# Chained instruction orders on four engines, and paired sums, in the delta-rule stage of a perceiver block

## The chip, the cores and the metric

The kernel runs on one core of a Trainium2 chip. The metric is device time in microseconds (us), the median of several runs. The engines are named as the profile names them: PE (TensorE; PEld is its weight loading), DVE (VectorE), ACT (ScalarE), POOL (GpSimd) and SP (SyncE, which here only issues DMAs).

## What is computed

`x` has 128 sequences of 32 tokens with 512 features, in all 4096 rows. Three blocks follow each other, each as `x = x + block(layernorm(x))`: a cross attention, a delta-rule layer with an MLP, and a quantised Hadamard feed-forward. The change touches the delta-rule layer, whose first half is, cut to what matters:

```python
h = _rms(x, attn_norm_w)
q = silu(silu(_causal_dwconv(h @ Wq.T, conv_q)))
k = silu(silu(_causal_dwconv(h @ Wk.T, conv_k)))
v = silu(silu(_causal_dwconv(h @ Wv.T, conv_v)))
q = _l2norm(q.reshape(B, T, nh, hd))     # 32 heads of 16
k = _l2norm(k.reshape(B, T, nh, hd))
beta = sigmoid(h @ Wbeta.T)
def step(S, inp):
    kt, qt, vt, bt = inp
    err = einsum('bhvk,bhk->bhv', S, kt) - vt
    S = S - bt[..., None, None] * err[..., None] * kt[..., None, :]
    o = einsum('bhvk,bhk->bhv', S, qt)
    return (S, o)
```

Then come an RMS norm, an output projection and an MLP of 1408 units.

## The kernel before, in words

**Stages.** Rows are handled in 8 groups (`NG`) of 512 rows (`SG`), that is, 16 sequences. `cross_attention` writes its result `x1` to DRAM. `delta_products` (L602) makes q, k, v, their products and lengths. `delta_out_mlp` (L923) makes the layer's output and the MLP in 16 blocks of 256 rows; `HadamardFfn` follows. The recurrence is not run token by token: within a sequence the products k·k and k·q of all token pairs are formed on PE, and a forward substitution over the 32 tokens (`Substitution.solve`, L513, on DVE) yields the vectors that the state would have been updated with. Products go to DRAM as `ld` (k·k) and `pd` (k·q, with the causal mask), values as `vd`, the solution as `ud`, the lengths of q as `rq`.

**A group's round.** `a_round` (L808) has twelve steps: k and q for each of four blocks of 128 channels, then v for the four. A step's parts are these. `channels` (L656): 4 matmuls into `pp` (three PSUM banks), an ACT copy with the last tap into `acc`, three DVE instructions for the other taps (L667). `activated` (L676): two SiLUs on ACT for the *preceding* step's `acc`; after a q step the pair k, q of that channel block is ready, and `masked` has two pieces of 256 rows queued. `hold` (L688): for up to three pieces ahead, eight DMAs on SP (`masked_operand`, L553, issued at L558) copy k and q head by head into one of three zeroed tiles `kqm`. `multiply` (L695), in eight of twelve steps (`due`): 32 PE instructions into the two `pg` banks, two ACT copies into `kk`, the mask on POOL, and POOL's DMAs to `ld` and `pd` (`products`, L561). In steps 3, 5, 7 and 9 ACT squares a pair, and in steps 4, 6, 8 and 10 `add` (L721) sums the squares by head on PE into three strips of 32 rows of the bank `pn`, the middle strip being the logits of beta. Step 11 takes roots and tanh (`lengths`, L731). In steps 7 to 10 `normed` (L647) normalises a tile of the next group on DVE (`hn`), transposes it on PE and copies it on ACT. For the group before, `behind_round` (L786) transposes lengths and beta (`by_tokens`, step 1) and values (`put_v`, steps 2 to 5), and inverts the lengths of q (`inverted`, steps 8 and 10; its load `rl` on SP at L594). `last_round` (L854) does the same for group 7, with the channels in the order k, v, q.

**Beside it.** `mixed` draws from the round and from the substitution in proportion to their estimated costs: `SHARE`, 24.3 us, per round, from group 1 on, the first 12.15 of it empty. `solve` loads a group's `ld` in four quarters into L (one buffer, 512 KB a quarter, L520) and `vd` into W (two buffers, L526). For each token there are a small product (L535), a product `pr` (L539) and a subtraction (L545), on 31 to 1 tokens. The rest of the substitution runs beside the MLP.

**Who orders.** The order in which an engine gets its instructions is fixed when the kernel is built: a scheduler takes them by program order, and may put a later one ahead when its own reckoning has the engine free. `InOrder` wraps an engine and ties each instruction that goes through it to the one before, so that their program order stays. Before the change PE and ACT are wrapped in this stage; DVE, SP and POOL are not. The matmul order, say, is therefore the written one, whereas a substitution step or a load can be put ahead of what is written before it.

**Start.** `scaled_rows` (L495) multiplies the 16 strips of `wk`, `wq`, `wv` and `wb` by the norm's weights on DVE (L502), written ahead of the first four `normed`. POOL zeroes the tiles `um` and `pe` of the next stage (L1528); `kqm` is zeroed on DVE, four strips a step (L831).

The lines that fix a step's order, from `a_round`:

```python
acc, last = channels(hT, n, ec)
with tc.issue_after(last):
    for _ in range(min(H4, len(blank))):
        nc.vector.memset(blank.pop(0), 0.0)
activated()
waiting.append((acc, dst, masked(ec) if n == "q" else kept))
if due[j] and count["done"] < len(held) and (old or j >= 4):
    multiply()
```

Of the kernel before, what the change touches and what calls it, by code (L numbers as in the profile page):

```python
# [494 lines left out]
def scaled_rows(nc, wp, name, norm, ws, engine=None):  # L495

    mul = engine.mul if engine else nc.vector.tensor_scalar_mul
    nw = wp.tile([P, DC], FP, name=name, bufs=1)
    nc.sync.dma_start(nw, norm.rearrange("(c p) -> p c", p=P))
    for t in ws:  # L500
        for dc in range(DC):
            mul(t[:, dc, :], t[:, dc, :], nw[:, dc : dc + 1])  # L502


class Substitution:
# [4 lines left out]
    def __init__(self, g, pool, ld, vd, ud):  # L510
        self.nc, self.pool, self.ld, self.vd, self.ud = g.nc, pool, ld, vd, ud

    def solve(self, gi):  # L513
# [5 lines left out]
        def load(s):  # L519
            nc.sync.dma_start(  # L520
                L[:, s : s + some].rearrange("p s h t -> p s (h t)"), rows[:, s : s + some]
            )
# [3 lines left out]
        nc.sync.dma_start(  # L526
# [5 lines left out]
        for s in range(T):  # L532
            if s % some == 0 and s + some < T:
                load(s + some)
            nc.vector.tensor_mul(w[:, s], w[:, s], bc(W[:, s, :, HD], HD))  # L535
            n = T - 1 - s
            if n:
                pr = self.pool.tile([P, T - 1, H4, HD], FP, name="pr")
                nc.vector.tensor_mul(  # L539
                    pr[:, 0:n],  # L540
                    bc(L[:, s, :, s + 1 : T].rearrange("p h t -> p t h"), HD),
                    w[:, s].unsqueeze(1).to_broadcast([P, n, H4, HD]),
                )
                yield 0.3 + 0.07 * n
                nc.vector.tensor_sub(w[:, s + 1 :], w[:, s + 1 :], pr[:, 0:n])  # L545
# [7 lines left out]
def masked_operand(nc, m, kq):  # L553


    for h in range(HH):
        rows = slice(h * HD, (h + 1) * HD)
        nc.sync.dma_start(m[rows, h % H4], kq[rows])  # L558
# [31 lines left out]
def inverted(nc, rq, r):  # L590
# [3 lines left out]
    nc.sync.dma_start(r, every)  # L594
    yield
    nc.vector.tensor_scalar_max(r, r, 1e-12)
    nc.vector.reciprocal(r, r)
# [4 lines left out]
def delta_products(  # L602
    g: Ctx, x1, stats, norm_w, wqT, wkT, wvT, conv_q, conv_k, conv_v, wbT, heads, causal, ld, vd,
    pd, rq, kd, beside,
# [16 lines left out]
    act = InOrder(tc, nc.scalar)  # L621
    with stack:
# [13 lines left out]
        scaled_rows(nc, wp, "nw", norm_w, [w["k"], w["q"], w["v"], w["b"]])  # L636

        kqm = [wp3.tile([P, H4, 2, KT], FP, name=f"kqm{i}") for i in range(3)]
        blank = [t[:, h] for t in kqm for h in range(H4)]
        mv, rs = stats  # L640

        def load(n):
            xt = xp.tile([P, D], FP, name="xt")
            nc.sync.dma_start(xt, x1[n * P : (n + 1) * P, :])
            return xt

        def normed(n, xt, hT):  # L647

            i = n % GT
            hn = hp.tile([P, D], FP, name="hn")  # L650
            nc.vector.tensor_scalar(
                hn, xt, mv[:, n, 0:1], rs[:, n, 1:2], ALU.subtract, ALU.mult
            )
            act.copy(hT[:, :, i * P : (i + 1) * P], g.transposed(ps, hn, g.ident, pe=pe))

        def channels(hT, n, ec):  # L656
# [9 lines left out]
            for d in range(1, TAPS):  # L666
                last = nc.vector.scalar_tensor_tensor(  # L667
# [3 lines left out]
            return acc.rearrange("p b t -> p (b t)"), last.ins  # L671
# [16 lines left out]
        def hold():  # L688
            while len(held) < min(len(pieces), count["done"] + len(kqm)):
                gi, ec, half, kq = pieces[len(held)]  # L690
                m = kqm[len(held) % len(kqm)]
                masked_operand(nc, m, kq[:, :, half * KT : (half + 1) * KT])
# [13 lines left out]
        class Group:  # L706

            def __init__(self, gi):  # L710
                self.gi = gi
                self.sums = psn.tile([3 * H, SG], FP, name="pn")
                self.v = {}

            def square(self, kq, of="kq"):
# [3 lines left out]
                return sq  # L719

            def add(self, sq, hT, ec, of="kq"):  # L721
                at = dict(start=ec == 0, stop=ec == DC - 1)
                if "k" in of:
                    pe.matmul(self.sums[0:H], hs[:, ec, :], sq[:, 0], **at)
                    pe.matmul(
                        self.sums[H : 2 * H], w["b"][:, ec, :], hT[:, ec, :], **at
                    )
                if "q" in of:
                    return pe.matmul(self.sums[2 * H :], hs[:, ec, :], sq[:, 1], **at)

            def lengths(self, of="kq"):  # L731

                if "k" in of:
                    f = self.factors = wk.tile([3 * H, SG], FP, name="f", bufs=1)
                    act.activation(f[H : 2 * H], self.sums[H : 2 * H], AF.Tanh, scale=0.5)
                for n, r in (("k", slice(0, H)), ("q", slice(2 * H, 3 * H))):
                    if n in of:
                        act.activation(self.factors[r], self.sums[r], AF.Sqrt)

            def by_tokens(self):  # L740
                f = self.factors
                pt = ps.tile([P, GT, 2 * H], FP, name="ps")
                for i in range(GT):
                    pe.transpose(
                        pt[:, i, :], f[0 : 2 * H, i * P : (i + 1) * P], g.ident[0 : 2 * H, 0 : 2 * H]
                    )
                self.n = st.tile([P, GT, H], FP, name="n")
                nc.vector.tensor_scalar_max(self.n, pt[:, :, 0:H], 1e-12)
                self.beta = st.tile([P, GT, H], FP, name="beta")
                nc.vector.tensor_scalar(self.beta, pt[:, :, H:], 0.5, 0.5, ALU.mult, ALU.add)  # L750
                n2 = st.tile([P, GT, H], FP, name="n2", bufs=1)
                nc.vector.tensor_mul(n2, self.n, self.n)
                nc.vector.reciprocal(n2, n2)
                nc.vector.tensor_mul(self.beta, self.beta, n2)

            def put_q(self):

                for c in range(DC):
                    rows = slice(2 * H + c * HH, 2 * H + (c + 1) * HH)
# [5 lines left out]
            def put_v(self, ec):  # L765
# [6 lines left out]
                nc.vector.tensor_mul(  # L772
# [13 lines left out]
        def behind_round(old, j):  # L786
# [4 lines left out]
            if j == 1:  # L791
# [3 lines left out]
                    nc, rq[old.gi], st.tile([P, P], FP, name="rl", bufs=1)  # L795
# [10 lines left out]
        loads = (2, 3, 4, 8)  # L806

        def a_round(gi, old, hT, made):  # L808
# [12 lines left out]
            for j, (n, ec) in enumerate(todo):  # L821
# [6 lines left out]
                acc, last = channels(hT, n, ec)  # L828
                with tc.issue_after(last):
                    for _ in range(min(H4, len(blank))):  # L830
                        nc.vector.memset(blank.pop(0), 0.0)  # L831
                activated()
                waiting.append((acc, dst, masked(ec) if n == "q" else kept))
                if due[j] and count["done"] < len(held) and (old or j >= 4):
                    multiply()
                if 3 <= j <= 9 and j % 2:
                    sq = new.square(kq[(j - 3) // 2])
                if 4 <= j <= 10 and j % 2 == 0:
                    new.add(sq, hT, (j - 4) // 2)
# [4 lines left out]
                if j == 11:  # L844
                    new.lengths()
                if 7 <= j <= 10:
                    normed((gi + 1) * GT + j - 7, xt[j - 7], hT_next)
# [6 lines left out]
        def last_round(gi, old, hT):  # L854
# [8 lines left out]
            for j, (n, ec) in enumerate((n, ec) for n in "kvq" for ec in range(DC)):  # L863
# [7 lines left out]
                acc, _ = channels(hT, n, ec)  # L871
                if (n, ec) == ("q", DC - 2):
                    left["q"] = [
                        i for i in nc.cur_bb.bb.instructions[before:] if i.engine == pe.last.engine
                    ][:1]
                activated()
                waiting.append((acc, dst, stored(ec) if n == "q" else kept))
                if count["done"] < len(held):
                    multiply()
                if 3 <= j <= 6:  # L880
                    new.add(sq, hT, j - 3, "k")
                if 2 <= j <= 5:
                    sq = new.square(kq[j - 2], "k")
                if j == 7:
                    new.lengths("k")
# [7 lines left out]
                if j == 11:  # L893
                    new.add(sq, hT, 0, "q")
                if j >= 10:
                    sq = new.square(kq[j - 10], "q")
# [3 lines left out]
            for ec in range(1, DC):  # L900
                if ec > 1:
                    sq = new.square(kq[ec], "q")
                sums = new.add(sq, hT, ec, "q").ins
                if ec > 1:
                    left["pe"].append(sums)
# [3 lines left out]

        hT = wk1.tile([P, DC, SG], FP, name="hT")  # L910
        for i in range(GT):
            normed(i, load(i), hT)
# [707 lines left out]
```

## Time and profile before

| what | value |
|---|---|
| runs, median of 3 | 2903.06 us (2902.81 to 2907.43) |
| profiled execution | 2912.17 us, of which the span is 2910.4 us |
| busy over the span | PE 2815.8 us (97%), PEld 1676.1, DVE 1995.4 (69%), ACT 1034.9 (36%), POOL 741.5 (25%) |
| granted PE clock, mean | 0.989 |
| first and last `pp` matmul | 686.3 and 1194.9 us |
| `pn` matmuls (sums and logits) | 192 instructions of 128x512, median 617 ns |
| substitution steps L539 and L545, whole span | 248 each, 307.6 and 308.1 us |

The span is the time from the first to the last instruction on the core. The time of an execution has a little around it. In a view's row, `out<-in` are the kernel's tile names, `xN` the number of instructions, and the bracket tells how long the engine stood idle before the row and whose end released it. A matmul of float32 takes two instructions, which is why a step's 4 matmuls appear as x8. A busy PE in the profile is not necessarily PE at full rate, since the ends of matmuls are modelled and the granted clock varies.

### The profile page before, as it was taken

The numbers are of one execution on the slowest core, as the hardware profiler recorded it, in microseconds if no ns is written. First come the engines' busy times: TensorE is split into PE (matmuls) and PEld (weight loads), VectorE is DVE, ScalarE is ACT, GpSimd is POOL, SyncE is SP. The second block draws the span as 40 slices with busy tenths as digits, with TensorE's granted clock in tenths as the row PEclk, the third lists the DMA queues.
The fourth block names the chain that finished last, engine by engine and source line by source line (L and its number), as shares of the span: only waits on it lengthen the run. The fifth ranks groups of instructions, "written<-read, shape, count | busy, mean of one in ns | idle before, by whom it ended". The sixth has DMA issues, their size and how long they took to land.

```text
span 2910.4 us, 44713 instructions
## 1 busy us (share of the span) xinstructions
PE 2815.8 (97%) x16726; PEld 1676.1 (58%) x16726; DVE 1995.4 (69%) x3355; ACT 1034.9 (36%) x1794; POOL 741.5 (25%) x1102
## 2 busy tenths in 40 slices
PE   8999999997999899999999999999999999999998
PEld 4444444443434344567666767776776756666665
DVE  2453544425599895678787878887722279999997
ACT  1111111213666466522212221211221147677665
POOL 2232323322777677221212111101000000000000
PEclk9999999998999899999999999999999999999999
DMA  9898998873555545841414141413231124444443
GB/s 317 268 321 296 345 334 291 302 248 87 163 161 144 167 135 155 236 137 57 131 57 132 57 132 54 123 59 94 69 112 33 35 73 83 90 88 82 87 81 71
DMA packets 347176, 429.77 MB, mean 148 GB/s; under 512 B 151888, under 2 KB 252624, under 8 KB 344528
## 3 DMA queue, kind: packets, MB, share of 16 engines
q1 hardware_dynamic: 305952, 324.36, 37.0%
q0 software_dynamic: 41008, 102.55, 11.6%
q8 instruction: 133, 2.18, 0.3%
q14 instruction: 83, 0.68, 0.1%
HBM read 288.88 MB, written 94.37 MB: 132 GB/s over the span
## 4 chain that ended last, share of the span: by engine, by line
PE 58%; DVE 11%; issue 2%; DMA 2%; POOL 2%; ACT 1%; SPq 1%; ACTq 0%; DVEq 0%; POOLq 0%
PE ps L151 18%; PE pm L1063 9%; PE pm L1052 9%; PE pm L1055 9%; PE pp L151 4%; PE ps L1026 4%; DVE W L545 3%; DVE acc L667 2%; DVE pr L539 2%; PE ps L995 2%; PE pg L151 1%; POOL kk L583 1%; DMA xs<-x 1%; SPq L558 1%; PE pn L151 1%
## 5 line engine op out<-in xcount | busy, mean ns | idle before, releaser
L1052 PE MATMUL pm<-hT,wg 128*128 128x256 f32 x1408 | 341.1, 385 | 0.2 <-ACT hT L1041 0.2
L1055 PE MATMUL pm<-hT,wu 128*128 128x256 f32 x1408 | 336.4, 382 | 1.8 <-DVE wu L1113 1.3
L539 DVE TENSOR_TENSOR pr<-L,W 128x1984 f32<-128x1984 f32 (+30 forms) x248 | 307.6, 1240 | 8.6 <-DMA L<-ld 4.0
L545 DVE TENSOR_TENSOR W<-W,pr 128x1984 f32<-128x1984 f32 (+30 forms) x248 | 308.1, 1242 | 2.9
L1063 PE MATMUL pm<-wd,mT 128*128 128x512 f32 x704 | 307.4, 592 | 0.0
L1055 PEld LDWEIGHTS pm<-hT,wu 128*128 128x128 f32 x1408 | 269.3, 192 | 39.7 <-DVE wu L1113 1.6
L1052 PEld LDWEIGHTS pm<-hT,wg 128*128 128x128 f32 x1408 | 261.9, 190 | 50.0 <-issue 12.0
L1063 PEld LDWEIGHTS pm<-wd,mT 128*128 128x128 f32 x704 | 132.4, 190 | 160.2 <-issue 160.0
L151 PE MATMUL ps<-wq,qT 128*128 128x512 bf16 x960 | 217.1, 379 | 3.0 <-ACT t L151 3.0
L1057 ACT ACTIVATE sg<-pm 128x256 f32<-128x256 f32 x176 | 67.0, 382 | 325.3 <-PE pm L1052 311.8
L1058 DVE TENSOR_TENSOR mT<-pm,sg 128x256 f32<-128x256 f32 x176 | 73.8, 419 | 156.4 <-PE pm L1055 152.0
L1389 POOL DMA_DIRECT2D xo<-x x31 | 26.3, 849 | 526.1 <-ACT xo L151 491.7
L323 POOL DMA_DIRECT2D vx<-vn x256 | 126.3, 500 | 119.5 <-DVE vn L319 84.3
L151 PEld LDWEIGHTS <-qT 128*128 128x128 bf16 x960 | 94.0, 98 | 103.7 <-issue 3.9
L151 DVE TENSOR_TENSOR mb<-m 128x1024 f32<-128x1024 f32 x128 | 153.2, 1217 | 0.1
L151 DVE TENSOR_TENSOR m<-mb 128x1024 f32<-128x1024 f32 x128 | 150.7, 1219 | 1.2
L579 POOL DMA_DIRECT2D ld<-kk x128 | 93.4, 729 | 151.2 <-ACT kk L151 121.4
L151 ACT ACTIVATE t<-ps,magic,qs 128x512 f32<-128x512 f32 x158 | 115.5, 780 | 46.0 <-DVE qs L151 42.2
L583 POOL TENSOR_TENSOR kk<-kk,cm 128x256 f32<-128x256 f32 x128 | 124.9, 976 | 2.7
L151 PEld LDWEIGHTS ps<-hd,mT 128*128 128x128 f32 x1024 | 120.8, 194 | 6.9 <-ACT mT L151 2.8
L151 PE MATMUL pp<-hT,wk 128*128 128x512 f32 x256 | 122.3, 622 | 1.5 <-DVE acc L667 0.8
L151 PE MATMUL ps<-hd,mT 128*128 128x128 f32 x1024 | 121.3, 277 | 2.3 <-ACT mT L151 2.3
(230 smaller groups left out, 4820.0 us busy)
## 6 DMA issues: line engine op xcount, KB each, us to landing
kall<-in_ctxT_dram SPq DMA_DIRECT2D x32, 2056.0 KB
cx<-in_ctx_dram SPq DMA_DIRECT2D x32, 2048.0 KB
x<-xo POOLq DMA_DIRECT2D x64, 256.0 KB, 3.5
ld<-kk POOLq DMA_DIRECT2D x128, 128.0 KB, 2.6
pd<-kk POOLq DMA_DIRECT2D x128, 128.0 KB, 2.6
L<-ld SPq DMA_DIRECT2D x32, 512.0 KB
pe<-pd SPq DMA_DIRECT2D x256, 64.0 KB
kqm<-kq SPq DMA_DIRECT2D x448, 32.0 KB
```

The costliest lines, as they stand in the source:

```text
L151: got = method(*args, **kw)
L323: nc.gpsimd.dma_start(vx[r : r + T, j, :], vn[j * T : (j + 1) * T, halves[h]])
L539: nc.vector.tensor_mul(pr[:, 0:n], bc(L[:, s, :, s + 1 : T].rearrange("p h t -> p t h"), HD), w[:, s].unsqueeze(1).to_broadcast([P, n, H4, ...
L545: nc.vector.tensor_sub(w[:, s + 1 :], w[:, s + 1 :], pr[:, 0:n])
L579: nc.gpsimd.dma_start(ld[r].rearrange("(i p) f -> p i f", p=P), kk[:, 0].rearrange("p i h t -> p i (h t)"))
L583: nc.gpsimd.tensor_mul(q, q, cm.unsqueeze(1).to_broadcast([P, 2 * H4, T]))
L1026: nc.tensor.matmul(pw, oT[:, i, dc, :], wo[:, dc, :], start=dc == 0, stop=dc == DC - 1)
L1052: nc.tensor.matmul(pg, wg[:, dc, fs], hT[:, dc, :], start=dc == 0, stop=dc == DC - 1)
L1055: nc.tensor.matmul(pu, wu[:, dc, fs], hT[:, dc, :], start=dc == 0, stop=dc == DC - 1)
L1057: nc.scalar.activation(sg, pg, AF.Silu)
L1058: mark[:] = [nc.vector.tensor_mul(mT[:, fc, :], pu, sg).ins]
L1063: nc.tensor.matmul(pd, mT[:, fc, i * P : (i + 1) * P], wd[:, fc, :], start=fc == 0, stop=fc == FC - 1,)
```

## The change

In `delta_products`, four things are done.

1. DVE and SP get an `InOrder` wrapper as well, and the substitution uses both wrappers while the stage runs. Every DVE instruction and DMA of the stage now keeps program order, substitution included.
2. The written order changes: `multiply` comes before `activated`, so on ACT the `kk` copies stand ahead of the SiLUs. `normed` is split: the DVE part moves to steps 6 to 9, transposes and copies (`turned`) stay in 7 to 10. The fourth load of a next tile moves from step 8 to 7.
3. Sums: the squares of two channel blocks are summed by one `add` in steps 6 and 10, in four strips of 32 rows (k and q, even and odd block). The logits get a bank of their own in step 11, four token tiles side by side (`logits`); `by_tokens` gets one more transpose and takes the maximum in two halves.
4. Start: the four `normed` come first; then `wk` and `wb` are scaled on DVE, `wq` on ACT, `wv` on DVE. The zeroing of `um` and `pe` goes from POOL to DVE, as twelve more strips of 512 elements among the steps 3 to 5 of the first round.

`last_round` is changed likewise. The diff, cut to its core:

```diff
     pe = InOrder(tc, nc.tensor)
     act = InOrder(tc, nc.scalar)
+    dve = substitution.dve = InOrder(tc, nc.vector)
+    sync = substitution.sync = InOrder(tc, nc.sync)
...
-        scaled_rows(nc, wp, "nw", norm_w, [w["k"], w["q"], w["v"], w["b"]])
+        nw = wp.tile([P, DC], FP, name="nw")
+        nc.sync.dma_start(nw, norm_w.rearrange("(c p) -> p c", p=P))
...
-        blank = [t[:, h] for t in kqm for h in range(H4)]
+        blank = [t[:, h] for t in kqm for h in range(H4)] + blanks
...
+            def add(self, ec, of="kq"):
+                if ec == 0 and "k" in of:
+                    self.sums = psn.tile([4 * H, SG], FP, name="pn")
+                for n in of:
+                    for r in range(2):
+                        at = (2 * "kq".index(n) + r) * H
+                        last = pe.matmul(
+                            self.sums[at : at + H], hs[:, ec + r, :], self.sq[r][:, "kq".index(n)],
+                            start=ec == 0, stop=ec == DC - 2,
+                        )
+                self.sq.clear()
+                return last
+
+            def logits(self, hT):
+                pb = ps.tile([P, P], FP, name="ps")
+                for dc in range(DC):
+                    for i in range(GT):
+                        pe.matmul(
+                            pb[i * H : (i + 1) * H], w["b"][:, dc, :], hT[:, dc, i * P : (i + 1) * P],
+                            start=dc == 0, stop=dc == DC - 1,
+                        )
+                self.tanh = st.tile([P, P], FP, name="tanh")
+                act.activation(self.tanh, pb, AF.Tanh, scale=0.5)
...
-        loads = (2, 3, 4, 8)
+        loads = (2, 3, 4, 7)
...
-                acc, last = channels(hT, n, ec)
-                with tc.issue_after(last):
-                    for _ in range(min(H4, len(blank))):
-                        nc.vector.memset(blank.pop(0), 0.0)
+                acc = channels(hT, n, ec)
+                for _ in range(min(H4, len(blank))):
+                    dve.memset(blank.pop(0), 0.0)
+                if due[j] and count["done"] < len(held) and (old or j >= 4):
+                    multiply()
                 activated()
                 waiting.append((acc, dst, masked(ec) if n == "q" else kept))
-                if due[j] and count["done"] < len(held) and (old or j >= 4):
-                    multiply()
                 if 3 <= j <= 9 and j % 2:
-                    sq = new.square(kq[(j - 3) // 2])
-                if 4 <= j <= 10 and j % 2 == 0:
-                    new.add(sq, hT, (j - 4) // 2)
+                    new.square(kq[(j - 3) // 2])
+                if j in (6, 10):
+                    new.add((j - 6) // 2)
...
                 if j == 11:
+                    new.logits(hT)
                     new.lengths()
                 if 7 <= j <= 10:
-                    normed((gi + 1) * GT + j - 7, xt[j - 7], hT_next)
+                    turned((gi + 1) * GT + j - 7, hn, hT_next)
+                if 6 <= j <= 9:
+                    hn = normed((gi + 1) * GT + j - 6, xt[j - 6])
...
         for i in range(GT):
-            normed(i, load(i), hT)
+            turned(i, normed(i, load(i)), hT)
+        for n, mul in (
+            ("k", dve.tensor_scalar_mul), ("b", dve.tensor_scalar_mul), ("q", act.mul),
+            ("v", dve.tensor_scalar_mul),
+        ):
+            scaled_rows(mul, w[n], nw)
...
+    substitution.dve, substitution.sync = nc.vector, nc.sync
...
-        for t in (*um, *pe):
-            nc.gpsimd.memset(t, 0.0)
```

## The prediction

> **What bounds the kernel now.** I read the page's chain first, then the busy time by stretch, then PE's waits, then the timeline around the two longest waits. PE carries the chain:
>
> ```profile
> PE 58%; DVE 11%; issue 2%; DMA 2%; POOL 2%; ACT 1%; SPq 1%; ACTq 0%; DVEq 0%; POOLq 0%
> ```
>
> The change touches one stage, so I cut it where a group's first `pp` product (k, channel block 0) starts on PE; a stretch is a "round" R0 to R7, of twelve steps each. Columns: stretch and its length, then busy time of PE, PEld, DVE, ACT, POOL with counts, granted clock, DMA share, GB/s.
>
> ```profile
> 686.29:744.58 58.29, 56.96 (x328) 23.93 (x328) 31.39 (x50) 31.99 (x52) 21.79 (x30) 0.97 0.33 87
> 744.58:805.90 61.32, 59.28 (x421) 25.57 (x413) 39.50 (x55) 39.51 (x65) 41.94 (x62) 1.00 0.60 171
> 805.90:870.84 64.94, 62.54 (x416) 26.73 (x412) 64.84 (x78) 40.35 (x66) 54.21 (x66) 0.97 0.57 157
> 870.84:936.69 65.85, 63.25 (x417) 26.74 (x413) 65.47 (x93) 40.50 (x66) 49.19 (x66) 0.97 0.53 148
> 936.69:1016.37 79.68, 64.57 (x417) 27.50 (x413) 71.42 (x98) 40.45 (x66) 54.09 (x67) 0.89 0.55 163
> 1016.37:1080.86 64.49, 60.87 (x417) 25.89 (x413) 61.77 (x83) 40.17 (x67) 49.76 (x66) 1.00 0.51 138
> 1080.86:1139.63 58.77, 58.77 (x417) 25.54 (x413) 33.13 (x52) 40.01 (x67) 47.40 (x70) 1.00 0.54 147
> 1139.63:1195.50 55.87, 55.11 (x282) 24.38 (x275) 36.06 (x59) 40.51 (x63) 30.09 (x51) 1.00 0.70 191
> ```
>
> R6 is the measure: the same work as R2 to R5 (PE x417), PE never idle, 58.77 us. There DVE has 33.13 us of work, none of it substitution. R2 and R3 last 6 to 7 us longer with DVE busy throughout. R1 to R5 exceed R6 by 2.6 + 6.2 + 7.1 + 20.9 + 5.7 = **42.4 us**. PE's waits in the stage (engine, line, releaser: total, times, longest):
>
> ```profile
> PE pg L151 <- ACT kk L151: 14.5, 13, 3.3
> PE pg L151 <- DMA kqm<-kq: 11.9, 2, 10.6
> PE ps L151 <- DVE hn L651: 9.9, 1, 9.9
> ```
>
> The first row is a chain of four: DVE puts pieces of substitution before a step's convolution (`acc` L667), ACT's SiLU waits for that `acc` (16.6 us of such waits in R3), the copy `kk<-pg` stands behind the SiLU on ACT, and PE needs the bank which that copy frees. The second is a flood; the third is the start (timelines of SP, PE and DVE; start, duration):
>
> ```profile
> 951.39 0.80 SPq L520 DMA_DIRECT2D L<-ld  x2
> 952.74 1.33 SPq L520 DMA_DIRECT2D L<-ld  x2
> 963.32 0.32 SPq L526 DMA_DIRECT2D W<-vd  x1
> 963.75 21.58 SPq L558 DMA_DIRECT2D kqm<-kq  x27
> 974.47 2.82 PE L151 MATMUL pg<-kqm,kq 64*32 64x256 f32 x32 [10.55 <-DMA kqm<-kq]
> 676.00 4.91 DVE L502 TENSOR_SCALAR wq<-wq,nw 128x512 f32<-128x512 f32 x4
> 683.67 1.94 PE L151 MATMUL ps<-ident,hn 128*128 128x128 f32 x8 [9.88 <-DVE hn L651]
> ```
>
> All four quarters of L (512 KB each) go out at once, W waits, and the `kqm` loads that PE needs come last on SP. After 10.55 us idle a product of 1.09 us takes 2.82.
>
> **The change, part by part.**
>
> *Start.* Now all 16 weight scalings precede the third `hn` on DVE, stretched by the POOL memsets (2.06 us for one scaling instead of 0.48). Afterwards the four `hn` come first, `wq` goes to ACT, the memsets leave POOL. The first transposes stay at 672.7 (they wait for the last attention tile); then two `hn` at 0.5, 0.85 of statistics, two transposes at 0.5 with copies at 0.58, and the first `pp` starts near 676.4, not 686.3: **-9.9**; the `wk` scalings (4 x 0.48) lie beside that. That first `pp` took 5.68 at half clock against 3.60; the gap on PE shrinks but does not vanish, so I take half of the difference: **-1.0** (bounds 0 and -2.1). `wq` on ACT: 4 x about 0.6 (a 128x512 ACT row takes 0.63), done while the first `pp` runs; without that cover 2.5 us. Twelve more memsets on DVE: 12 x 0.485 = 5.8 us in R0, where DVE is busy 31.4 of 58.3.
>
> *Sums of two chunks.* PE rows (`pn` start, next row; then two neighbours with four column tiles):
>
> ```profile
> 776.69 0.62 PE L151 MATMUL pn<-sq,hs 128*32 128x512 f32 x1
> 777.68 3.70 PE L151 MATMUL pp<-hT,wq 128*128 128x512 f32 x8
> 653.83 2.15 PE L336 MATMUL ps<-kall,qT 128*32 128x289 f32 x32
> 1180.92 1.50 PE L995 MATMUL ps<-pe,um 128*32 128x128 f32 x42
> ```
>
> Three products side by side cost 0.99 us, four times a round. Afterwards four side by side, twice. That four run at once L336 shows: an instruction of 512 columns costs 0.43 (`pp`, 8 in 3.44), so one of 289 costs 0.243, and 32 would take 7.8 us one after the other, not 2.1. I take 1.03 for each. The logits become 16 products, 32 instructions; at L995's 1.50/42 = 36 ns that is 1.1. With 0.1 for the added transpose 3.96 becomes 3.27, **-0.7** a round; bounds: -1.1 (all at L336's rate of 3.7 at once) and +1.2 (the four no better than two by two, 4 x 0.99). R0 to R6: **-4.9**. In R7 eight additions of 0.95 become four plus logits, -2.6, of which I take **-2.0** because the last stand in the tail. The Trainium skill, "TensorE: Matmul & The Clock Gate", section "The mechanism", speaks against this: a weight load overlaps a running matmul only where the row groups differ, and column tiles share theirs; its section "Measured speedup vs the span model" has 2.38x for three column tiles. By that, three cost 2.56/2.38 = 1.08 and four perhaps 1.4, an estimate from that page, and the sum would shrink by some 6 us. The trace has 0.99 for three.
>
> *ACT order.* `kk` now goes before the SiLUs. It no longer waits for DVE; behind it wait two SiLUs, 1.3 us later than now. For them wait `kq`, the `kqm` loads and `square`, needed a step (4.9 us) or more later: nothing. Sqrt and tanh shrink on ACT, busy 40 of 59: nothing.
>
> *DVE order.* Substitution is dealt out evenly: 24.3 us of estimated cost per round from the middle of R1 to R7, instead of as early as possible. The rows L539, L545 and L535 sum to 70.4 + 70.9 + 15.4 = 156.7 us over the stage, over 6.5 rounds 24.1 each. DVE's own part is 33.1 (R6) or, saturated, 65.5 - 37.8 = 27.7 (R3). So 52 to 57 of 58 us: it fits, barely. Between two convolutions now stands about one piece, at most 2.2 us, and three `pp` banks and ACT's 2 to 3 us per step give room. `hn` is made a step before its transposes, so PE does not wait for it.
>
> *SP order.* L's quarters now go out one by one, eight substitution steps apart: the flood goes. The rest keeps program order; 64 `kqm` issues take 43.8 us in R6, with `xt`, `rl` and L about 47.5 of 58. A wait (`W` for the stores of `vd`, L for the last read of the solve before, `xt` for `hn`) now holds the `kqm` loads behind it; these have three buffers, some 20 us of lead. POOL's queue is not chained; its stores come no later.
>
> So R1 to R5 lose their 42.4. I give back 0.5 in R1 and 1.0 in each of R2 to R6 for coupling at 90 to 99% of DVE, and 3.0 in R7, where DVE gets 24 us on top of 36.1 in 55.9.
>
> **Sum.** -9.9 - 1.0 - 4.9 - 2.0 - 42.4 + 5.5 + 3.0 = **-51.7 us**. The profiled execution took 2912.2 (span 2910.4, 1.8 around it), so 2860.5; it lies 9.1 above the median of the runs, 2903.1, which gives **2851**. The stages behind are bound by PE (95 to 100% busy by stretches of 100 us) and take over the same state of the substitution, so I let them move as a block.
>
> **Rivals.**
> 1. *DVE becomes the bound.* For: 33.1 + 24.1 = 57.2 of 58, and a chained DVE cannot pass a blocked instruction. Against: R3's saturated 27.7. Rounds of 62 instead of the mean 65.8 in R1 to R6 save 23; R7 grows by 6; with 10.9 at the start and 0.7 in R0: -28.6, **2874**.
> 2. *The order does not change in effect*, and only start and sums count: -10.9 - 6.9, **2885**. Against: none of the stage's substitution runs after 1080.86 today, so its order must change.
> 3. *Slower: SP in order.* A blocked load ahead of `kqm`. Slack is 58.1 - 47.5 = 10.6 us a round; beyond that each microsecond of waiting is one of PE at `pg`. To undo 51.7 over seven rounds it takes 7.4 a round, so it decides from 18 us of blocking; at 20 us a round it is 7 x 9.4 - 51.7 = +14, **2917**. For: SP's waits in the stage reach 12.5 us for one load (`rl`), 9.1 for W. Against: `rl` is written seven steps after its data are stored.
>
> **Numbers.** Forecast 0.57, rival 1 0.22, rival 2 0.06, rival 3 0.11, within 0.2% (5.8 us, about what a measurement can tell) 0.04. Faster 0.85, same 0.04, slower 0.11. Range: below, all 42.4 kept, the full clock term and the best sums: -9.9 - 2.1 - 7.7 - 2.6 - 42.4 = -64.7, 2838. Above it must reach rivals 1 and 2: 2886. Left out are rival 3, no change and the edges.
>
> **What would show it.** Start: first `pp` near 676.4. Sums: two `pn` bundles a round of 1.03, logits 1.1. Order: rounds R2 to R6 of 58 to 59.5 with DVE at 52 to 57 in each, no wait of `pg` for `kqm` above 2 us, and less than 3 us in all for `kk`. It is wrong if DVE is busy throughout in rounds above 61, if SP's waits sit in front of `kqm` loads that PE waits for, or if the stages after the last `pp` get longer by as much as this one gets shorter.

## The result, and the profile after

| | median us (range) | runs |
|---|---|---|
| before | 2907.63 (2902.81 to 2914.64) | 12 |
| after | 2892.59 (2882.31 to 2897.80) | 12 |

The ratio is **0.9942** (95% interval 0.9930 to 0.9954): faster, by 15 us and not by 52. The forecast was 2851, its range 2838 to 2886. The profiled execution went from a span of 2910.4 to one of 2891.7 us.

First the chain's shares by engine, in the page of after. PE still carries it:

```profile
PE 56%; DVE 6%; DMA 2%; issue 1%; ACT 1%; POOL 1%; SPq 0%; DVEq 0%; ACTq 0%; POOLq 0%
```

Next the stage cut into the rounds R0 to R7, as before: stretch and length, busy time of PE, PEld, DVE, ACT and POOL with counts, granted clock, DMA share, GB/s.

```profile
674.28:733.62 59.34, 56.30 (x353) 24.24 (x353) 39.24 (x67) 35.78 (x58) 21.77 (x30) 0.97 0.35 95
733.62:801.33 67.71, 61.65 (x441) 27.57 (x438) 36.15 (x55) 39.93 (x65) 44.25 (x65) 0.95 0.58 163
801.33:861.87 60.54, 59.08 (x442) 26.42 (x438) 55.84 (x67) 39.84 (x65) 51.24 (x64) 1.00 0.52 141
861.87:925.77 63.90, 60.33 (x441) 27.00 (x437) 62.34 (x77) 40.06 (x65) 50.29 (x65) 0.97 0.54 147
925.77:987.76 61.99, 59.34 (x442) 26.34 (x438) 60.21 (x90) 39.94 (x65) 45.90 (x65) 1.00 0.54 150
987.76:1053.81 66.05, 61.01 (x441) 27.30 (x437) 53.89 (x78) 40.05 (x65) 47.99 (x66) 0.95 0.60 181
1053.81:1117.00 63.19, 60.73 (x441) 27.28 (x437) 56.04 (x71) 39.84 (x65) 52.12 (x65) 0.97 0.59 164
1117.00:1175.00 58.00, 55.42 (x303) 25.40 (x300) 56.35 (x81) 39.19 (x61) 33.28 (x47) 0.97 0.69 194
```

The round of 79.68 us is gone. But no round has the 58 to 59.5 us that was forecast for R2 to R6, and R6, undisturbed before, is now 63.19. An undisturbed round after the change takes 57.75 us (two of an experiment below, where PE is never idle), so R1 to R6 exceed six of those by 383.4 - 346.5 = 36.9 us. Before, the same excess over 58.77 was 42.4. The old excess went, and nearly as large a new one came. The longest of PE's waits in the stage shows which:

```profile
PE pg L151 <- DMA kqm<-kq: 14.2, 10, 3.0
```

No row for `kk` is left (14.5 before), nor the 9.9 for `hn` at the start. Instead `pg` waits for `kqm` ten times. Going through the steps of each round, 25.4 of the 36.9 us lie in the fifth to seventh step, where the first products of new keys and queries stand, and 6.7 in R1's last two. The start and the sums came as forecast (start, duration; `x8` counts instructions):

```profile
674.28 5.40 PE L151 MATMUL pp<-hT,wk 128*128 128x512 f32 x8 [1.91 <-ACT hT L151]
706.56 1.07 PE L151 MATMUL pn<-sq,hs 128*32 128x512 f32 x8
732.61 1.08 PE L151 MATMUL ps<-hT,wb 128*32 128x128 f32 x32
```

The first `pp` starts 12.0 us earlier, still slow: its 5.40 us have a granted clock of 0.68, where later ones take 3.60. Four sums side by side cost about 1.0, the logits 1.1.

### The profile page after: what moved, and what is told of

It reads as the page before. It is cut to its first block, busy times and chain, and to the rows that moved or that the text cites. A ratio compares the mean times of both kernels' runs of the same rounds, so it can differ in the third digit from the quotient of the medians.

```text
span 2891.7 us, 45038 instructions
## 1 busy us (share of the span) xinstructions
PE 2800.2 (97%) x16863; PEld 1679.6 (58%) x16926; DVE 2013.4 (70%) x3371; ACT 1036.8 (36%) x1791; POOL 741.8 (26%) x1098
## 4 chain that ended last, share of the span: by engine, by line
PE 56%; DVE 6%; DMA 2%; issue 1%; ACT 1%; POOL 1%; SPq 0%; DVEq 0%; ACTq 0%; POOLq 0%
PE ps L151 18%; PE pm L1084 10%; PE pm L1087 9%; PE pm L1095 9%; PE ps L1058 4%; PE pp L151 3%; PE ps L1027 2%; DVE W L541 1%; DVE pr L535 1%; PE pg L151 1%; DVE m L151 1%; DMA xs<-x 1%; DVE mb L151 0%; SPq L151 0%; PE ps L97 0%
## 5 line engine op out<-in xcount | busy, mean ns | idle before, releaser
L535 DVE TENSOR_TENSOR pr<-L,W 128x832 f32<-128x832 f32 (+30 forms) x199 | 237.1, 1191 | 7.1 <-DMA L<-ld 3.1
L541 DVE TENSOR_TENSOR W<-W,pr 128x832 f32<-128x832 f32 (+30 forms) x199 | 239.6, 1204 | 2.4
```

The costliest lines, as they stand in the source:

```text
L535: self.dve.tensor_mul(pr[:, 0:n], bc(L[:, s, :, s + 1 : T].rearrange("p h t -> p t h"), HD), w[:, s].unsqueeze(1).to_broadcast([P, n, H4, ...
L541: self.dve.tensor_sub(w[:, s + 1 :], w[:, s + 1 :], pr[:, 0:n])
```

## The experiments

Each ratio is to the kernel before; 0.001 is 2.9 us. The stage is told by its first and last `pp` in the profiled execution (starts of their rows), and by what the span has behind that:

| kernel | ratio (95%) | first `pp` | first to last | behind |
|---|---|---|---|---|
| before | 1 | 686.3 | 505.6 | 1718.5 |
| after | 0.9942 (0.9930, 0.9954) | 674.3 | 497.3 | 1720.2 |
| products a step later | 0.9901 (0.9883, 0.9918) | 674.0 | 480.2 | 1721.2 |
| VectorE's order free | 1.0018 (1.0008, 1.0028) | 675.3 | 526.2 | 1720.1 |
| SP's order free | 0.9920 (0.9902, 0.9938) | 670.1 | 486.0 | 1729.3 |
| orders alone | 0.9991 (0.9974, 1.0008) | 683.3 | 500.5 | 1722.4 |
| rows in place | 0.9875 (0.9857, 0.9892) | 678.5 | 476.2 | 1721.9 |
| the same, share 0.23 | 0.9927 (0.9909, 0.9946) | 674.1 | 471.9 | 1747.6 |
| the same, share 0.25 | 0.9893 (0.9881, 0.9906) | 675.3 | 476.0 | 1721.1 |
| share 0.23, pace 52 | 0.9893 (0.9879, 0.9907) | 676.3 | 468.6 | 1729.4 |
| share 0.23, pace 60 first | 0.9914 (0.9898, 0.9929) | 672.2 | 465.3 | 1731.9 |

### The slack of kqm: where the new wait comes from

The theory was read from timelines. Before the change, in R6 (which starts at 1080.86), the second SiLU of the first q block, SP's first `kqm` load for it, and PE's products with it:

```profile
1094.31 0.63 ACT L151 ACTIVATE kq<-acc 128x512 f32<-128x512 f32 x1
1094.96 11.62 SPq L558 DMA_DIRECT2D kqm<-kq  x18
1101.88 1.12 PE L151 MATMUL pg<-kqm,kq 64*32 64x256 f32 x32
```

SP starts 0.02 us after the SiLU has ended, and 6.9 us later the product runs without a wait, just in time. After the change, in R2 (from 801.33), where the SiLU ends at 816.95:

```profile
816.32 0.63 ACT L151 ACTIVATE kq<-acc 128x512 f32<-128x512 f32 x1
816.97 10.34 SPq L151 DMA_DIRECT2D kqm<-kq  x16
...
823.66 1.07 PE L151 MATMUL pg<-kqm,kq 64*32 64x256 f32 x24 [0.60 <-DMA kqm<-kq]
```

The SiLU now ends 15.62 us into the round and not 14.08, since the copy `kk<-pg` stands ahead of it, and the product, which PE reaches at the same place as before, has to wait. The three buffers are no lead here: the loads can't be issued before their data exist. R1, R4 and R6 have the same SiLU end and first waits of 0.51 to 0.60 us; in R3, where it ends 0.5 us later still, the wait is 1.92.

R5 (from 987.76) is the costliest round. Its SiLU ends 15.62 us into the round too, at 1003.38:

```profile
1003.40 13.13 SPq L151 DMA_DIRECT2D kqm<-kq  x16
...
1011.00 0.64 PE L151 MATMUL pg<-kqm,kq 64*32 64x256 f32 x8 [2.08 <-DMA kqm<-kq]
1014.60 1.93 PE L151 MATMUL pg<-kqm,kq 64*32 64x256 f32 x24 [2.96 <-DMA kqm<-kq]
...
1017.37 3.08 PE L151 MATMUL pp<-hT,wq 128*128 128x512 f32 x4
```

PE, which would have gone on at 1008.92, waits 2.08 and then 2.96 more, and the next `pp` begins slowly (3.08 us for half of eight instructions that elsewhere take 3.60). The SiLU's order explains only a part of this. From the SiLU's end to the end of the `pp` before the product, R2 and R5 differ in the share of the DMA engines' time that is in use, the last column but one (the columns are those of the table of rounds):

```profile
816.95:822.42 5.47, 5.47 (x16) 2.29 (x14) 5.33 (x8) 2.79 (x4) 5.18 (x5) 1.00 0.43 114
1003.38:1008.92 5.54, 5.54 (x16) 2.29 (x14) 5.37 (x10) 2.90 (x4) 5.43 (x10) 1.00 1.02 418
```

In R5 a quarter of L and a whole W go out shortly before the SiLU's end (998.50 and 998.93) and a store of `ud` just after it (1004.22), and SP needs 7.95 us for the first eight `kqm` loads, where R2 needs 5.14. So 5.0 of the 14.2 us of waits lie in a round whose loads are also slowed by other transfers; 7.8 lie in the other rounds from R1 on, and 1.4 in R0. No run here takes those transfers away, so their share is read from the trace and not tested.

**SiLU ahead of the products.** Edit, in `a_round`:

```diff
-                if due[j] and count["done"] < len(held) and (old or j >= 4):
-                    multiply()
                 activated()
                 waiting.append((acc, dst, masked(ec) if n == "q" else kept))
+                if due[j] and count["done"] < len(held) and (old or j >= 4):
+                    multiply()
```

> The changed kernel with the two SiLUs of a step put back ahead of the product and its kk copies in the ordinary rounds; every other order as changed (PE, DVE and SP get the same sequences, only ACT's differs). Theory A (the kqm loads start only when a q's SiLU ends, and the change moved that SiLU behind the kk copies, so that the products of steps 4 and 5 wait for their operand): the operand is ready 1.5 us earlier, the excess of steps 4 and 5, 25 us over rounds 1 to 6 in the changed kernel, falls to 10 to 16, and the time falls 5 to 12 us under the changed kernel, ratio to before 0.990 to 0.9925. Theory B (SP, kept in program order, holds the kqm loads behind blocked loads): SP's order is the same, so no change beyond 3 us, ratio 0.993 to 0.9955.

Ratio 0.9929 (0.9910 to 0.9948), span 2885.7. The waits of `pg` for `kqm` fell from 14.2 to 6.9 us, five times in place of ten, so the order on ACT is about half of that wait. Outside R0 and R5 they fell from 7.8 to 1.4, but in R5, where the DMA engines are full again, 4.1 of 5.0 us stay. New waits for `hn` took 9.4 us. In time the gain can't be told from none.

**Products a step later.** The list of steps that multiply, with the first pieces of a round's own keys moved from the fifth to the sixth step:

```diff
-        due = (0, 1, 1, 0, 1, 1, 0, 1, 1, 0, 1, 1)
+        due = (1, 1, 0, 0, 0, 1, 1, 0, 1, 1, 1, 1)
```

> The changed kernel with the eight products of a round in steps 0, 1, 5, 6, 8, 9, 10, 11 instead of 1, 2, 4, 5, 7, 8, 10, 11: the first new operand has one step (4 to 5 us) more between its SiLU and its product, and ACT's order stays kk first. Theory A: no product waits for kqm by more than 1 us, steps 4 to 6 lose their excess, the time falls by 15 to 25 us under the changed kernel, ratio 0.985 to 0.989. Theory B: the SP queue is as blocked as before, less than 8 us, ratio 0.991 to 0.9945. A third theory (DVE, busy 60 of 62 us in some rounds, is the bound): less than 8 us too, but with no wait of a product for kqm left and DVE busy throughout.

Ratio 0.9901 (0.9883 to 0.9918): 12 us faster than the changed kernel, in a stage 17 us shorter, and between the ranges of the theories. The longest of PE's waits in the stage:

```profile
PE ps L151 <- DVE hn L151: 17.1, 10, 4.0
```

and one of the ten in the timeline:

```profile
954.67 0.66 PE L151 MATMUL ps<-ident,hn 128*128 128x128 f32 x4 [2.76 <-DVE hn L151]
```

The wait for `kqm` is down to 1.5 us, all of it in R5: the due list of the changed kernel leaves no room for a later SiLU, and that is the first layer of what was missed. A second appears below it. In R3 and R4 the eighth and ninth step now take 6.15 to 7.23 us where 3.97 and 5.05 are undisturbed: the normalized rows come late from DVE, which works on the substitution.

**Both.** The two edits together:

```diff
-        due = (0, 1, 1, 0, 1, 1, 0, 1, 1, 0, 1, 1)
+        due = (1, 1, 0, 0, 0, 1, 1, 0, 1, 1, 1, 1)
...
                 activated()
                 waiting.append((acc, dst, masked(ec) if n == "q" else kept))
+                if due[j] and count["done"] < len(held) and (old or j >= 4):
+                    multiply()
```

> Both edits: SiLUs first and the products in steps 0, 1, 5, 6, 8, 9, 10, 11. Theory A: the supply has slack already with the later products, so the SiLU order adds nothing: within 3 us of the run with the later products alone; if ACT's copies behind the SiLUs matter (the gain the prediction gave to that order), it is 3 to 10 us slower than that run, with waits of products for kk.

Ratio 0.9882 (0.9862 to 0.9902). The interval overlaps that of the later products alone, so the order of the SiLU is not shown to add anything once the products are later; the waits for `kk` did not come back (1.2 us).

### The four orders

**SP's order free.**

```diff
-    sync = substitution.sync = InOrder(tc, nc.sync)
+    sync = substitution.sync = nc.sync
```

> The changed kernel with SP taken out of the chain (its loads may be reordered again); the rest as changed. Theory A: steps 4 and 5 keep their excess of about 25 us; only the xt load that came late in round 1 (10.6 us for one step there) can come earlier, so 0 to 7 us under the changed kernel, ratio 0.992 to 0.9945. Theory B: the loads pass the blocked ones, steps 4 and 5 become clean, and the time falls by 20 us or more, ratio under 0.988.

Ratio 0.9920 (0.9902 to 0.9938), overlapping that of after. The waits for `kqm` stay at 14.2 us, so they are not made by SP's order. The eleventh step of R1 shrinks from 10.63 to 8.11: in the changed kernel R1's fourth `xt` load stands on SP behind L, W and eight `kqm` loads, goes out at 788.76, and `hn` waits 6.35 us for it (4.24 here). The profiled stage is 11.3 us shorter than in the changed kernel, but the stretch behind it 9.1 us longer. (POOL's stores were never chained; only SP's DMAs were.)

**VectorE's order free.**

```diff
-    dve = substitution.dve = InOrder(tc, nc.vector)
+    dve = substitution.dve = nc.vector
```

> The changed kernel with VectorE's order given back to the planner, the three other engines' orders kept. Theory A (the hand-written order holds the substitution's pieces to their share of each step, and that took the 16 us excess of one round away): the pieces crowd into one round again, waits for kk or hn come back on TensorE, ratio 0.997 to 1.003. Theory B (the order on VectorE is what makes instructions queue behind the pieces and costs more than it holds): no crowd in any round, ratio 0.986 to 0.991.

Ratio 1.0018 (1.0008 to 1.0028): 22 us slower than the changed kernel, as the first theory said. The substitution's instructions on DVE, by stretch (those of tile W; the third, fourth and fifth round; busy time behind the comma, with counts):

```profile
811.08:880.17 69.09, 39.74 (x32) 0.93 0.49 134
880.17:943.97 63.80, 24.96 (x32) 0.97 0.50 137
943.97:1009.84 65.87, 8.42 (x21) 0.97 0.56 159
```

The planner crowds 39.7 us of it into one round and 8.4 into another; PE waits 25.1 us for `hn`. The order on DVE does what it says: in the changed kernel R2 to R7 hold 25.2, 29.6, 28.8, 21.9, 23.2 and 24.3 us.

**Orders alone.** The changed kernel with sums and start put back (the edits of the next two runs together):

```diff
+                if 4 <= j <= 10 and j % 2 == 0:
+                    new.add(sq, hT, (j - 4) // 2)
...
+        for n in "kqvb":
+            scaled_rows(dve.tensor_scalar_mul, w[n], nw)
...
+        for t in (*um, *pe):
+            nc.gpsimd.memset(t, 0.0)
```

> The four orders alone: the changed kernel with the start and the sums as they were before. Theory A (the parts add up: start 11 us, sums 7 us by the two runs that undo one of them, so of the 17 us nothing is left for the orders): ratio 0.9995 to 1.003. Theory B (the orders gained by themselves, and start and sums gained little beside them): 0.995 to 0.998.

Ratio 0.9991 (0.9974 to 1.0008), just below the first theory's range: nothing that can be measured. So start and sums carry the gain; the orders give with one hand (DVE, 22 us against the planner's) and take with the other (`kqm`).

### Sums and start

**Sums one by one.** `add`, `logits`, `lengths` and `by_tokens` as in the kernel before:

```diff
-                if j in (6, 10):
-                    new.add((j - 6) // 2)
+                if 4 <= j <= 10 and j % 2 == 0:
+                    new.add(sq, hT, (j - 4) // 2)
```

> The changed kernel with the sums of one chunk at a time again and the logits in sixteen instructions behind them, as before; the four orders kept. Theory A (TensorE sets each round's length, so the 0.7 us of its work that the pairs took out come back whole): 5 to 8 us slower than the changed kernel, ratio 0.9960 to 0.9970. Theory B (TensorE waits some us for kqm in the fifth and sixth step of each round, and a sum that stands in those steps lies partly beside the transfers): 0 to 3 us, ratio 0.9935 to 0.9952.

Ratio 0.9966 (0.9954 to 0.9978), 7 us slower than the changed kernel: the sum's rows give the right price, and the waits beside them did not hide it.

**Start as before.** Scalings ahead of the first rows, all on DVE; `um` and `pe` cleared by POOL:

```diff
+        for n in "kqvb":
+            scaled_rows(dve.tensor_scalar_mul, w[n], nw)
...
+        for t in (*um, *pe):
+            nc.gpsimd.memset(t, 0.0)
```

> The changed kernel with the start as it was: all weights scaled by VectorE, the operands of the last stage cleared by GpSimd ahead of the first round, the query weights in the same order on VectorE. Theory A (the stage's first projection came 12.0 us earlier and nothing behind it gives that back): 10 to 13 us slower than the changed kernel, ratio 0.9978 to 0.9990. Theory B (part of it comes back, since the clears now lie on VectorE in R0 and R0 took 1.05 us more): 6 to 9 us, ratio 0.9962 to 0.9974.

Ratio 0.9980 (0.9966 to 0.9994), 11 us slower: nothing behind the start gives its gain back.

### VectorE's load, the layer below

**Rows in place.** On top of both edits of the first part, the next group's rows are normalized in the tile that they were loaded into. That frees room for five such tiles, and the loads and the normalization come earlier:

```diff
-            hn = hp.tile([P, D], FP, name="hn")
-            dve.tensor_scalar(hn, xt, mv[:, n, 0:1], rs[:, n, 1:2], ALU.subtract, ALU.mult)
-            return hn
+            dve.tensor_scalar(xt, xt, mv[:, n, 0:1], rs[:, n, 1:2], ALU.subtract, ALU.mult)
+            return xt
...
-        loads = (2, 3, 4, 7)
+        loads = (0, 1, 2, 3)
...
-                if 6 <= j <= 9:
-                    hn = normed((gi + 1) * GT + j - 6, xt[j - 6])
+                if 5 <= j <= 8:
+                    normed((gi + 1) * GT + j - 5, xt[j - 5])
```

> The kernel of the run before with SiLU ahead of the products and the later due list (0.9882 of before), and with the next group's rows read, normalized and transposed in one tile: five tiles in place of three and two, loaded in steps 0 to 3 (not 2, 3, 4 and 7), normalized in steps 5 to 8 (not 6 to 9). Theory A (what is left is the order of DVE: the normalized rows reach TensorE's transposes 2 to 4 us late, 15.4 us of waits in that run, and in R1 one load is late by 6 us behind a slow one): these waits go, with them the half clock behind them, 10 to 18 us; ratio 0.982 to 0.985. Theory B (VectorE is at its limit in R2 to R5, 60 of 62 us busy, and whatever is taken out of its way comes back at another tile): the waits for hn go and waits for W, acc or pp come in their place; ratio 0.987 to 0.989.

Ratio 0.9875 (0.9857 to 0.9892), the fastest kernel here, 19 us below the changed one and 36 below before. The waits for `hn` are gone, and R1 takes 57.80 us in place of the 64.08 of both edits (67.71 in the changed kernel), so the late load was that round's trouble. But beside the run of both edits nothing measurable was won, as the second theory had it: R3 to R5 still take 62.0, 62.2 and 64.5 us with DVE 60 us busy, and short waits for `kk` (5.3 us) and `kqm` (3.3) are back.

**Share 0.23.** One size: less substitution beside each round.

```diff
-SHARE = 0.27 * SOLVE
+SHARE = 0.23 * SOLVE
```

> The kernel with rows in place (0.9875 of before) with one size changed: the substitution's share of a round is 0.23 of a solve, not 0.27, so that 15% of its pieces, some 4 us of VectorE a round, move behind the stage. Theory A (VectorE is the bound of R2 to R5 and R7: 22 to 29 us of substitution beside 33 of its own in rounds that TensorE alone would do in 57.9): these rounds shrink by 1 to 3 us each; ratio 0.983 to 0.9855. Theory B (VectorE is busy but sets nothing, or the stage behind, which takes the pieces over, becomes longer by as much): 0.9865 to 0.9895.

Ratio 0.9927 (0.9909 to 0.9946), 15 us slower than with 0.27; outside both ranges. R3 in the table of stretches (R4 takes 57.75 us):

```profile
846.65:904.41 57.76, 57.76 (x442) 26.14 (x438) 55.32 (x70) 39.72 (x65) 48.56 (x65) 1.00 0.58 158
```

and the longest of PE's waits behind the stage:

```profile
PE ps L1026 <- POOL um L1008: 22.3, 4, 6.7
```

R1 to R5 take 57.8 to 58.4 us and PE hardly stands: VectorE's load was the second layer, and 55.5 us of work on it fit in a round where 60 do not. What was saved there is paid behind: the solves end later, and four of the next stage's blocks wait 4.6 to 6.7 us each for `um`, which is filled from them. R6 still takes 63.5 us, with a wait of 2.8 us for ACT in its first step that was not followed up.

**Share 0.23 in the changed kernel**, without the other edits:

```diff
-SHARE = 0.27 * SOLVE
+SHARE = 0.23 * SOLVE
```

> The changed kernel (0.9942 of before) with the substitution's share at 0.23 in place of 0.27 and nothing else. Theory A (its first limit is the kqm loads that land too late in the fifth and sixth step, and VectorE's load is only the layer below): waits of pg for kqm stay at 10 to 15 us, ratio 0.991 to 0.9945. Theory B (VectorE's load alone makes the rounds long): ratio below 0.990.

Ratio 0.9992 (0.9977 to 1.0006). Both theories missed the time, because both left out the stage behind, where `um` costs 23.2 us here too. Of what they said on the stage, the first held only in part: the waits for `kqm` fell to 7.9 us, and R2 to R6 took 59.2 to 63.2.

**Rows in place, share 0.23, SP's order free.** On top of that kernel:

```diff
-    sync = substitution.sync = InOrder(tc, nc.sync)
+    sync = substitution.sync = nc.sync
```

> The kernel with rows in place and the share at 0.23, with SP's order given back to the planner. Theory A (a load that waits in SP's fixed order holds those behind it, 6 us in the changed kernel's profile, but with rows loaded in steps 0 to 3 and products due later nothing waits for them any more): no difference from the run with SP's order fixed, within 0.002. Theory B (SP's order still costs): 0.002 to 0.004 faster than that run.

Ratio 0.9927 (0.9909 to 0.9944), the same as with SP's order fixed. With loads early and products late, that order costs nothing.

**The pace behind the stage.** Three more kernels ask whether the price is a date or VectorE's time: share 0.23 with 60 units in place of 45 beside each of the next stage's first four blocks, share 0.23 with 52 beside every block, and share 0.25 with 45. All three stand on the rows in place.

```diff
-                return [(PACE, part(all_u, PACE))]
+                pace = 60.0 if b < 4 else PACE
+                return [(pace, part(all_u, pace))]
```

> Rows in place and the share at 0.23 (0.9927 of before), with the pieces that this moves behind the stage taken up at once: 60 instead of 45 units of substitution beside each of the first four blocks of the next stage. Theory A (the stage did gain from the smaller share, and the price is a deadline: TensorE waits 22.3 us in four blocks for um, whose u comes from a solve that is now finished too late): the waits for um go, ratio 0.983 to 0.987. Theory B (VectorE is the price there too: 15 units more beside a block make its own chain late): waits for um shrink and others take their place, ratio 0.989 to 0.993.

```diff
-PACE = 45.0
+PACE = 52.0
```

> Rows in place and the share at 0.23, with 52 instead of 45 units beside every block of the next stage. Theory A (a deadline): the waits for um are shorter from block to block as the solves catch up by 7 units a block, 22 us become 10 to 14; ratio 0.987 to 0.990. Theory B (VectorE): no gain, 0.991 to 0.994.

```diff
-SHARE = 0.27 * SOLVE
+SHARE = 0.25 * SOLVE
```

> Rows in place (0.9875 of before with the share at 0.27, 0.9927 at 0.23), the share at 0.25, half way. Theory A (a deadline: at 0.25 the first solves are ready just about in time, so the rounds gain and the next stage does not pay): 0.984 to 0.987. Theory B (each microsecond taken out of the stage comes back behind it at a fixed rate): 0.9890 to 0.9912.

Ratios 0.9914 (the second theory's range), 0.9893 (the first's) and 0.9893 (the second's), with the intervals in the table. The waits for `um` go with pace 60, and with 52 only one of 4.6 us stays: that was a date. None of the three beats the share of 0.27, though. With pace 60 DVE is busy 277.8 us of the 300 from 1170 to 1470, against 228.9 with rows in place alone, and what the stage wins (10.9 us, first to last `pp`) is lost behind it (9.9). That profile is of the fastest of the kernel's six runs (2871.2 us, median 2881.0), while that of the rows in place is of its slowest (2878.4, median 2871.5), so in a typical run more is lost than the two profiles show. Which wait carries that loss behind the stage was not settled: PE's named waits there differ by a few us, the rest is spread.

## Why the prediction was wrong

| term | forecast | measured |
|---|---|---|
| start, with its clock | -10.9 | -12.0 in the trace, 2.9 of it from ahead of the stage; undoing it costs 11 (6 to 16) |
| sums, R0 to R7 | -6.9 | undoing them costs 7 (2 to 12) |
| orders: -42.4, give back 5.5 and 3.0 | -33.9 | -2.6 alone (-7.6 to +2.3) |

**The start** was right in size, its place by luck: 674.28 against 676.4. The prediction kept the first transposes at 672.7. They started at 669.83, since the attention stage ended earlier; over the runs with the new start that time lies between 665.7 and 674.2, so 2.9 of the 12.0 us are not the change's. From there to the first `pp` it took 4.45 us, where 3.7 were forecast and 13.6 stood before: a gain of 9.1. The half of the clock term that I took did not come (5.40 against 5.68).

**The sums** were right. The undisturbed round went from 58.77 to 57.75, 1.0 where 0.7 was forecast, and the bundles cost what the rows had said. The estimate of perhaps 1.4 us for four column tiles, worked out from the 2.38x that the Trainium skill, "TensorE: Matmul & The Clock Gate", "Measured speedup vs the span model", has for three, did not hold: the trace has 1.07 for eight instructions of 512 columns in four strips, so the measurement decides against a loss there.

**The step that failed is the one that costed the ACT order at nothing**: "For them wait `kq`, the `kqm` loads and `square`, needed a step (4.9 us) or more later: nothing", with its counterpart under SP, "these have three buffers, some 20 us of lead". The delay itself was right (1.3 us forecast, 1.5 measured). The lead was not. It holds for a load whose data exist; the first pieces of a round's own queries become loadable when the SiLU ends, 6.9 us ahead of their product, and before the change that was enough by about 0.5 us (an estimate: in R6 the product's ninth instruction ran 7.18 us after the SiLU's end, and in R2 of the changed kernel it could run 6.71 after it). I had the row that shows it, R6 with no wait at all, and read "no wait" as "room". In place of nothing the order cost 6.4 us of waits for `kqm` outside R0 and R5, those that went when the SiLUs stood first again. Moving the products one step later, which helps R5 too, took 12 us (6 to 18) of the time away.

Under SP, "the flood goes" held only in part: no wait of 10.55 us is left, but in R5 L, W and `ud` still fill the DMA engines (share 1.02) while PE waits 5.04 us.

**A second step failed below it**: "52 to 57 of 58 us: it fits, barely", with 24.1 us of substitution in each round. The mean was right, the dealing is not so even: 25.2, 29.6, 28.8, 21.9, 23.2, 24.3 in R2 to R7, so that R3 and R4 have 60 to 62 us of DVE's work for 57.75 of PE's. That is one of the prediction's own signs of being wrong: in R3 DVE is busy 62.34 of 63.90 us. In a DVE that keeps program order, the rows for the next group stand behind those pieces. This is the first rival, as a layer and not as the bound of the whole stage. That 55.5 us fit without a wait is shown by the run with a share of 0.23.

**A third was not seen at all**: that all of the 42.4 us could simply go. With the rows in place 18.9 us of excess are left in R1 to R6, and the stretch behind is hardly longer (1721.9), so more than half could. The rest goes with VectorE's work: where a share of 0.23 took it out of the rounds, the stretch behind became 8 to 29 us longer than with the rows in place alone, and at a share of 0.25 the stage itself won nothing.

**The rivals.** The second, an order without effect, came nearest in time (2885 against 2892.6) and is wrong in mechanism: the order on DVE is worth 22 us against the planner's. The third, SP in order, is seen in one place only, R1's late `xt`; the `kqm` loads that PE waits for were not held on SP by a blocked load, but by their own data and, in R5, by full DMA engines. The stages behind moved as a block (1718.5 and 1720.2), as forecast.

## What to carry to other kernels

A row without a wait says nothing of how much room there is: measure slack from the producer's end to the consumer's start, along the whole path (SiLU, issue, landing), before costing a delay at nothing. When an engine's order is fixed by hand, count its work per round, not as a mean over the stage: here 60 us of it beside PE's 57.75 made rounds of 62 to 64.5 us. And excess that comes from real work does not all vanish by arranging it better; ask where that work will stand instead, and who needs its result by when.

## What the runs showed of the hardware that was not expected

Two short waits close together cost PE more than themselves. In R5 of the changed kernel waits of 2.08 and 2.96 us have 0.64 us of work between them, and four of a `pp`'s instructions behind them took 3.08 us, 0.77 each against the 0.45 of eight in 3.60; the granted clock was 0.50 from 1014.60 to 1017.37. A single wait of 2.76 us (954.67, with the products a step later) left the next `pp` at 3.60.

SP's issue takes time of its own: eight `kqm` loads took 5.1 us to issue in a quiet round, so the last of a piece's loads is late by the queue alone. With the DMA engines full it took longer: 16 loads in 13.13 us in R5, 0.82 each and up to 1.41 for one, against 10.34 in R2, 0.65 each.
